# A spectral convolution stage: the next unit's column transforms spread one to a convolution group, with a third PSUM bank, reordered stores and an earlier start

## The chip, the cores and the metric

The kernel runs on one core of one Trainium2 chip. The metric is the device time of one execution in microseconds (us). The median of three executions of the kernel before is 3194.32 us (3190.97 to 3194.67). TensorE is called PE here, VectorE DVE, ScalarE ACT, GpSimd POOL and SyncE SP, as in the profile.

## The reference

Four residual layers act one after the other on x, of shape 8 x 32 x 256 x 256 (batch, channel, height, width), in fp32:

```
x = x + conv0(gn(x))   # spectral: rfft2, mix 32 low and 32 high modes, irfft2, + bias
x = x + conv1(gn(x))   # one 5x5 kernel, each channel on its own, padding 2
x = x + conv2(gn(x))   # a gated recurrence over the 256 columns
x = x + conv3(gn(x))   # running maxima in four directions, then a 1x1 convolution
```

`gn` normalises pairs of channels over the whole image, so a pair's mean and variance must be known before the next layer can use it. The change lies in one function, `inverse_and_conv`, which does the inverse transform of layer 0, adds it to x, takes the statistics of the sum, does layer 1 (the 5x5 convolution) and takes the statistics for layer 2.

## The kernel before, in words

`inverse_and_conv` works through 16 **units** `u`: one image and 16 of its 32 channels each, split in two halves `ch` of 8 channels. A half lives in one of five SBUF buffers `x1_0` to `x1_4`, taken in rotation by `(2u + ch) % 5` (line 340). A buffer has nine column blocks `p` of 32 columns (28 new ones and a rim), and the width is on partitions in four quarters `a` of the image's height.

What a unit needs, step by step:

- `load(u, i)` (381): POOL issues DMAs that fetch x in three pieces of three blocks, two DMAs (one a half) of 768 KB each.
- `load_spectrum(b)` (352): SP issues four DMAs that fetch an image's mixed modes. `spectrum(b)` (362) adds the mean's terms to them on DVE, with one small matmul into the PSUM tag `st`.
- `over_rows` (400): the inverse transform over rows, four calls a unit of 8 PE records in the trace each, PSUM tag `s`; ACT copies the result to `tt`.
- `transform(u, p)` (582) calls `over_columns` (416): the inverse transform over columns for block p, 16 PE records (L424) into two tiles of PSUM tag `up` (two banks), which DVE adds to x (L433) into the x1 buffers. After blocks 2, 5 and 8 it issues the next piece of x for a later unit.
- `squares` (441) and `scale` (452): sums of squares (mostly on ACT), a matmul over them, and on POOL the power that gives the factor `r` of layer 1's normalisation.
- `conv(u, ch, g)` (475): the 5x5 convolution of one channel pair, 36 PE records (L490) into three of four PSUM banks of tag `vp`; five DVE operations (L527) multiply by `r`, add x and sum. A unit has eight such **groups** `g`, four to a half.
- `squares2` (532), `statistics` (552), `keep` (575): layer 2's statistics.
- `store(u, ch)` (541): SP writes a finished half to `x2d` in DRAM in 36 DMAs, four quarters `a` (outer loop) by nine blocks `p` (inner), rows of 256 bytes. Of the very last half, POOL issues 16.

The order of the work is written out by hand (`manual_schedule`, 596): every engine runs its instructions in the order of the program text. Between the groups of unit u stand the column transforms of unit u+1, placed by the tuple

```
PLACES = ((0,), (1, 2), (3, 4), (5, 6), (7,), (8,), (), ())
```

so two transforms follow each other after groups 1, 2 and 3, with a little other PE work between them, and none follows groups 6 and 7. The row transforms of unit u+2 follow groups 3 to 6. `scale(u+1, 0)` comes at the end of unit u. The spectrum of a later image is fetched after group 7 of odd units and prepared after group 2 of the next unit. SP has one queue: stores and spectrum fetches start in program order. A buffer may be overwritten by a later unit's L433 only when the store of its earlier contents has landed: unit u+1's second half takes over the buffer of unit u-1's first half.

After the stage, `recurrence` (672) starts with the transpose of the statistics (L695) and reads `x2d`.

Of the kernel before, what the change touches and what calls it, by code (L numbers as in the profile page):

```python
# [23 lines left out]
A = 4  # L24
# [3 lines left out]
NT = 9  # L28
# [272 lines left out]
def inverse_and_conv(tc, k, d, smd, xmean, x2d, stb, first):  # L301
# [12 lines left out]
    BANKS = ((0, 2), (2, 6), (6, 9))  # L314
    PIECES = ((0, 3), (3, 6), (6, 9))

    PLACES = ((0,), (1, 2), (3, 4), (5, 6), (7,), (8,), (), ())
    with ExitStack() as ctx:
        one = ctx.enter_context(tc.tile_pool(name="a2c", bufs=1))
        xp = ctx.enter_context(tc.tile_pool(name="a2x", bufs=1))  # L320
# [76 lines left out]
                r=[None, None],  # L397
            )

        def over_rows(u, c, tag="s", bufs=1):  # L400


            b, h = units[u]
            tp = ps.tile([P, 2, H], F32, name=f"tp_{u}_{c}", tag=tag, bufs=bufs)
            for j in range(2):
                for ch in range(2):
                    nc.tensor.matmul(
                        tp[64 * ch : 64 * ch + 64, j],
                        lhsT=specs[b][:, 2 * CH * h + CH * ch + c + j].rearrange("p r y -> p (r y)"),
                        rhs=k.eh,  # L410
                        start=True,
                        stop=True,
                    )
            nc.scalar.copy(state[u]["tt"][:, :, c : c + 2, :], tp.rearrange("p c (a q) -> p a c q", a=A))

        def over_columns(u, p, tag="up", bufs=2):


            tt = state[u]["tt"]
            ups = [ps.tile([P, CH * Q], F32, name=f"up_{u}_{p}_{ch}", tag=tag, bufs=bufs) for ch in range(2)]  # L420
            for a in range(A):
                for ch in range(2):
                    r = slice(64 * ch, 64 * ch + 64)
                    nc.tensor.matmul(  # L424
                        ups[ch][32 * a : 32 * a + 32],
                        lhsT=k.gw[r, p, :],
                        rhs=tt[r, a].rearrange("p c q -> p (c q)"),
                        start=True,
                        stop=True,
                    )  # L430
            for ch in range(2):
                free(
                    nc.vector.tensor_tensor(  # L433
                        x1_of(u, ch)[:, p, :, 1 : 1 + Q],
                        ups[ch].rearrange("p (c q) -> p c q", q=Q),
                        xs.pop((u, ch, p)),
                        ALU.add,
                    )
                )
# [32 lines left out]
            if some[0]:  # L472
                tc.declare_no_dep(ins.ins, group="conv", reason="later matmuls of the same bank end last")

        def conv(u, ch, g):

            vps = [
                ps.tile([P, 2 * (hi - lo), Q], F32, name=f"vp_{u}_{ch}_{g}_{lo}", tag="vp", bufs=4) for lo, hi in BANKS
            ]

            def tiles(bank, kind, start=False, stop=False, signal=False, wait=None):
                lo, hi = BANKS[bank]
                for i, r in enumerate(pairs):
                    o = pairs[i if kind == 0 else 1 - i]
                    to = pairs[i if (kind == 0) != (bank == 1) else 1 - i]
                    ins = nc.tensor.matmul(  # L490
                        vps[bank][to],
                        lhsT=k.conv[r, P : P + 64] if kind == 2 else k.conv[r, o],
                        rhs=pair_of(u, ch, g, lo, hi, (2, 0)[i] if kind == 2 else 1, r),
                        start=start,
                        stop=stop,
                    )
                    if wait is not None and i == 0:
                        ins._wait_ge(sem, wait)
                if signal:
                    ins.then_inc(sem, 1)  # L500
                    count[0] += 1
                    tc.add_to_no_dep_group("conv", ins.ins)
                    tc.no_tile_sem_insts.add(ins.ins.name)
                    some[0] = True
                return count[0]

            tiles(1, 1, start=True)
            tiles(2, 1, start=True)
            second = tiles(2, 2, signal=True)
            first = tiles(1, 2, signal=True)  # L510
            tiles(0, 1, start=True)
            tiles(2, 0, stop=True, wait=second)
            third = tiles(0, 2, signal=True)
            tiles(1, 0, stop=True, wait=first)
            tiles(0, 0, stop=True, wait=third)
            s1 = state[u]["s1"]
            everywhere, r1 = slice(0, P), state[u]["r"][ch]
            for n, lo, hi, src, o, rows in (
                (3, 6, 9, vps[2], everywhere, everywhere),
                (2, 2, 6, vps[1], pairs[1], pairs[0]),  # L520
                (2, 2, 6, vps[1], pairs[0], pairs[1]),
                (0, 0, 1, vps[0][:, 0:2], everywhere, everywhere),
                (1, 1, 2, vps[0][:, 2:4], everywhere, everywhere),
            ):
                x = pair_of(u, ch, g, lo, hi, rows=rows)
                free(
                    nc.vector.scalar_tensor_tensor(  # L527
                        x, src[o], r1[rows, g : g + 1], x, ALU.mult, ALU.add, accum_out=s1[rows, 0, n, ch, g : g + 1]
                    )
                )  # L530
# [10 lines left out]
        def store(u, ch):  # L541
            b, h = units[u]
            c0 = 2 * CH * h + CH * ch
            for a in range(A):
                for p, t in enumerate(BLOCKS):
                    lo, hi = 0 if t == 0 else 2, 32 if t == NT - 1 else 30
                    (nc.gpsimd if 2 * u + ch == 2 * n - 1 and p % 2 else nc.sync).dma_start(  # L547
                        out=x2d[b, a, c0 : c0 + CH, TS * t + lo : TS * t + hi].rearrange("c w q -> w c q"),
                        in_=x1_of(u, ch)[32 * a + lo : 32 * a + hi, p, :, 1 : 1 + Q],
                    )  # L550
# [28 lines left out]
                    by_pair(stb[:, kind, b, 2 * CH * h : 2 * CH * (h + 1)]), twice(st[:, kind], 2)  # L579
                )  # L580

        def transform(u, p, again):
            if u:
                over_columns(u, p)
            else:
                over_columns(u, p, "vp", 4)
            if p == 0:
                for ch in range(2):
                    squares(u, ch, 0, 0, 1)
            if again < n:  # L590
                for i, (_, hi) in enumerate(PIECES):
                    if p == hi - 1:
                        load(again, i)

        n = len(units)
        with tc.manual_schedule(engines=None):
# [5 lines left out]
            for u in range(2):  # L602
                begin(u)
            for c in range(0, CH, 2):
                over_rows(0, c, *(("s", 1), ("up", 2))[c // 2 % 2])
            for p in range(NT):
                transform(0, p, 1)
                if p % 2:
                    over_rows(1, p - 1)
                if p == 4:  # L610
                    for ch in range(2):
                        squares(0, ch, 1, 1, 5)
            for ch in range(2):
                squares(0, ch, 2, 5, NT, ch == 1)
                scale(0, ch, 3)
            for u in range(n):
                for g in range(2 * G):
                    conv(u, g // G, g % G)
                    places = PLACES[g] if u + 1 < n else ()
                    for p in places[:1]:  # L620
                        transform(u + 1, p, u + 2)

                    if g == 1 and u > 0:
                        scale(u, 1)
                    if g == 2 and u > 0:
                        st = statistics(u - 1)
                    if g == G - 1 and u + 2 < n:
                        begin(u + 2)
                    if G - 1 <= g < 2 * G - 1 and u + 2 < n:
                        over_rows(u + 2, 2 * (g - G + 1))  # L630
                    for p in places[1:]:
                        transform(u + 1, p, u + 2)
                    squares2(u, g // G, g % G)
                    if g == 2:
                        if u > 0:
                            keep(u - 1, st)
                        if u % 2 == 0 and u + 2 < n:
                            spectrum(units[u + 2][0])
                    if g == 5 and u + 1 < n:
                        squares(u + 1, 0, 1, 1, NT)  # L640
                    if g == 7 and u % 2 and u + 3 < n:
                        load_spectrum(units[u + 3][0])
                    if g % G == G - 1 and (u, g) != (n - 1, 2 * G - 1):
                        store(u, g // G)
                    if u == n - 1 and g == G:
                        nc.gpsimd.dma_start(out=flat(first[:, 0 : B - 1]), in_=first_columns(x2d, 0, B - 1))
                if u + 1 < n:
                    scale(u + 1, 0)
                    squares(u + 1, 1, 1, 1, NT)
            keep(n - 1, statistics(n - 1))  # L650
            store(n - 1, 1)
# [537 lines left out]
```

## Time and profile before

| what | value |
|---|---|
| median of three executions | 3194.32 us |
| the profiled execution | 3195.71 us |
| its span, first to last instruction | 3193.9 us |
| around the span | 1.8 us |
| convolution stage, first column transform to last store issue | 333.6 to 1160.0 us |
| PE busy in 440 to 940 us | 469.57 of 500 us |
| DVE busy in 440 to 940 us | 351.39 of 500 us |
| ACT busy in 440 to 940 us | 293.77 of 500 us |
| mean busy share of the 16 DMA engines in 440 to 940 us | 0.78 |
| DMA share in 1085 to 1125 us, after the last load of x | 0.51 |

How to read it: the profile is of one execution, so sums are made against 3195.71 us. A busy share tells how much of a stretch an engine worked, not whether it set the pace. Time in which SP only waits is not in these rows, so SP has to be read from the order and spacing of its DMA issues.

### The profile page before, as it was taken

How to read it: one execution, taken by the hardware profiler on the slowest of the kernel's cores; microseconds unless marked ns; L12 is line 12 of the kernel's file. 1: busy time of each engine (PE TensorE's matmuls, PEld its weight loads, DVE VectorE, ACT ScalarE, POOL GpSimd, SP SyncE). 2: the span in 40 equal slices, each digit the busy share in tenths (PEclk: the TensorE clock that was granted, in tenths of full speed). 3: DMA queues.
4: the chain of work that ended last, by engine and by line, in shares of the span. 5: the costliest groups of instructions: out<-in, count | busy, mean ns of one | idle time of the engine just before them, and what ended most of it. 6: DMA issues, size and time to landing. Idle time of an engine off the chain costs nothing.

```text
span 3193.9 us, 112013 instructions
## 1 busy us (share of the span) xinstructions
PE 2870.8 (90%) x47802; PEld 1672.7 (52%) x47802; DVE 2589.1 (81%) x5188; ACT 1856.4 (58%) x4362; POOL 862.3 (27%) x1241
## 2 busy tenths in 40 slices
PE   7985799999989969999999999999999678888887
PEld 4655344444434436666666666666666423333333
DVE  5752577777767748999999999999999799999997
ACT  3432365665646657888888888888888412222222
POOL 0110011111111035555555555555555400000000
PEclk9985899999999989999999999999999889999998
DMA  9977577788777655555566655555565588888885
GB/s 384 388 284 200 131 180 202 183 195 196 189 183 184 143 144 142 145 144 145 150 157 160 160 146 146 147 146 146 154 160 134 128 323 321 328 329 329 327 327 233
DMA packets 527057, 655.75 MB, mean 205 GB/s; under 512 B 388824, under 2 KB 389736, under 8 KB 500828
## 3 DMA queue, kind: packets, MB, share of 16 engines
q1 hardware_dynamic: 483628, 494.33, 54.4%
q0 software_dynamic: 17200, 85.05, 8.3%
q10 hardware_dynamic: 25728, 69.21, 5.5%
q8 instruction: 374, 6.13, 0.8%
q14 instruction: 127, 1.04, 0.1%
HBM read 371.63 MB, written 272.63 MB: 202 GB/s over the span
## 4 chain that ended last, share of the span: by engine, by line
PE 60%; DVE 24%; DMA 5%; issue 4%; SPq 4%; ACT 2%; POOL 0%; DVEq 0%; ACTq 0%; POOLq 0%
PE r L742 13%; PE z L742 12%; PE vp L490 8%; PE ni L742 6%; PE nh L742 6%; DVE x L527 4%; DVE rv L1001 4%; PE up L424 4%; SPq L547 3%; PE yp L131 2%; DVE dq L1007 2%; DMA x2d<-x 2%; DVE uq L1009 2%; DVE m L1015 2%; DVE m L1013 2%
## 5 line engine op out<-in xcount | busy, mean ns | idle before, releaser
L750 PE MATMUL z<-hs,weights 64*64 64x256 f32 x4080 | 539.4, 382 | 0.0
L750 PE MATMUL r<-hs,weights 64*64 64x256 f32 x4080 | 525.1, 375 | 0.0
L750 PE MATMUL ni<-hs,weights 64*64 64x256 f32 x4080 | 524.9, 375 | 0.0
L832 POOL TENSOR_TENSOR xw<-xw,hs 128x256 f32<-128x256 f32 x496 | 340.6, 687 | 634.0 <-DVE hs L831 634.0
L527 DVE SCALAR_TENSOR_TENSOR x<-vp,r,x 64x512 f32<-64x512 f32 (+2 forms) x640 | 351.1, 564 | 162.9 <-PE vp L490 136.2
L490 PE MATMUL vp<-x,c_conv 64*64 64x384 f32 (+2 forms) x4608 | 455.7, 513 | 0.2
L1047 ACT ACTIVATE ot<-o,bres 128x512 f32<-128x512 f32 x256 | 155.1, 688 | 505.3 <-PE o L1032 490.3
L826 POOL TENSOR_TENSOR a<-zm,xn 128x256 f32<-128x256 f32 x510 | 373.3, 732 | 6.5 <-issue 6.3
L824 ACT ACTIVATE n<-n,bih 128x256 f32<-128x256 f32 x510 | 259.2, 508 | 185.8 <-DVE n L823 185.8
L490 PEld LDWEIGHTS vp<-x,c_conv 64*64 64x64 f32 x4608 | 237.5, 137 | 232.3 <-issue 126.3
L742 PE MATMUL z<-xn,weights 64*64 64x256 f32 x2040 | 305.3, 376 | 24.1 <-ACT xn L722 24.1
L1032 PE MATMUL o<-m,wsc 32*32 32x512 f32 x3072 | 226.0, 716 | 110.8 <-DVE m L1015 104.0
L742 PE MATMUL r<-hs,weights 64*64 64x256 f32 x2040 | 319.1, 389 | 4.4 <-DVE hs L831 3.4
L742 PE MATMUL r<-xn,weights 64*64 64x256 f32 x2040 | 305.5, 376 | 1.3 <-ACT rs L817 1.3
L742 PE MATMUL nh<-xn,weights 64*64 64x256 f32 x2040 | 305.7, 376 | 0.0
L742 PE MATMUL ni<-hs,weights 64*64 64x256 f32 x2040 | 305.2, 375 | 0.0
L742 PE MATMUL z<-hs,weights 64*64 64x256 f32 x2040 | 305.2, 376 | 0.0
L722 ACT ACTIVATE xn<-xw,shift,turned 128x256 f32<-128x256 f32 x496 | 290.5, 586 | 0.1
L750 PEld LDWEIGHTS ni<-hs,weights 64*64 64x64 f32 x4080 | 284.5, 133 | 0.3
L818 DVE SCALAR_TENSOR_TENSOR n<-nh,bhh,rs 128x256 f32<-128x256 f32 x510 | 246.3, 483 | 45.7 <-ACT rs L817 31.2
L750 PEld LDWEIGHTS r<-hs,weights 64*64 64x64 f32 x4080 | 281.0, 131 | 0.2
L817 ACT ACTIVATE rs<-r,brz 128x256 f32<-128x256 f32 x510 | 241.6, 474 | 53.5 <-PE r L750 31.9
(164 smaller groups left out, 6271.1 us busy)
## 6 DMA issues: line engine op xcount, KB each, us to landing
xb<-in_xl_dram POOLq DMA_DIRECT2D x96, 768.0 KB, 6.5
xa<-in_xt_dram SPq DMA_DIRECT2D x64, 1024.0 KB
x<-x3d SPq DMA_DIRECT2D x32, 2048.0 KB
fw<-fwd SPq DMA_DIRECT2D x32, 2048.0 KB
out_dram<-ot ACTq DMA_DIRECT2D x64, 1024.0 KB
xw<-x2d SPq DMA_DIRECT2D x31, 2048.0 KB
fwd<-fm SPq DMA_DIRECT2D x248, 256.0 KB
x3d<-xw SPq DMA_DIRECT2D x248, 256.0 KB
```

What stands on the lines that cost most here:

```text
L490: ins = nc.tensor.matmul(vps[bank][to], lhsT=k.conv[r, P : P + 64] if kind == 2 else k.conv[r, o], rhs=pair_of(u, ch, g, lo, hi, (2, 0)[i] ...
L527: nc.vector.scalar_tensor_tensor(x, src[o], r1[rows, g : g + 1], x, ALU.mult, ALU.add, accum_out=s1[rows, 0, n, ch, g : g + 1])
L722: nc.scalar.activation(norms[bi][:, b, w], raws[bi][:, b, w], AF.Identity, bias=shift[:, b : b + 1], scale=sc[:, 1, b : b + 1])
L742: ins = nc.tensor.matmul(out[r], lhsT=weights[r, kind, gate, :], rhs=src[r], start=start, stop=stop)
L750: ins = nc.tensor.matmul(out[pairs[1 - i]], lhsT=weights[r, kind, gate, :], rhs=prev[r, :, q0 : q0 + Q], start=False, stop=stop,)
L817: rs = nc.scalar.activation(r, p["r"], AF.Sigmoid, bias=brz[:, 0:1])
L818: nc.vector.scalar_tensor_tensor(m, p["nh"], bhh[:, 2:3], r, ALU.add, ALU.mult)
L824: nc.scalar.activation(m, m, AF.Tanh, bias=bih[:, 2:3])
L826: product = nc.gpsimd.tensor_tensor(a, zm, cur, ALU.mult)
L832: nc.gpsimd.tensor_tensor(raw, raw, new, ALU.add)
L1032: nc.tensor.matmul(pts[b2][i][32 * j : 32 * j + 32].rearrange("p (w q) -> p w q", q=Q), lhsT=wsc[q, b2, t, :], rhs=src[j][q, b2], start=first,
L1047: nc.scalar.activation(ot[:, i], pts[b2][i], AF.Identity, bias=bres[:, b2, i : i + 1])
```

## The change

1. The `up` tag gets three banks in place of two; the tag `s` goes away, and `over_rows` shares the one bank of `st` with the small statistics matmuls.
2. Of unit u+1, transform 0 is issued at the end of group 7 of unit u-1; transforms 1, 2, 3, 5, 6, 7, 8 follow groups 0 to 6 of unit u, and transform 4 stands inside group 3, before the last quarter or so of its matmuls (`between`).
3. `scale(u, 0)` moves from the end of unit u-1 into group 0 of unit u, at the same place inside the group.
4. The squares of unit u+1's first half come in three parts (block 0 after group 1, blocks 1 to 5 after group 4, blocks 6 to 8 before group 7) instead of two; the second half keeps two.
5. `store` loops over blocks outside and quarters inside. Number, size and engine of its DMAs stay as they were.
6. `load_spectrum` moves from after group 7 of odd units to after group 2, and `spectrum` from after group 2 of even units to after group 7 of the odd unit before. `keep` moves from group 2 to group 3.
7. The first `scale`s and transform 0 of unit 1 are put in the same order ahead of unit 0.

```diff
-    PLACES = ((0,), (1, 2), (3, 4), (5, 6), (7,), (8,), (), ())
+    PLACES = (1, 2, 3, 5, 6, 7, 8)
...
-        def over_rows(u, c, tag="s", bufs=1):
+        def over_rows(u, c, tag="st", bufs=1):
...
-        def over_columns(u, p, tag="up", bufs=2):
+        def over_columns(u, p, tag="up", bufs=3):
...
-        def conv(u, ch, g):
+        def conv(u, ch, g, between=()):
...
             third = tiles(0, 2, signal=True)
+            for work in between:
+                work()
             tiles(1, 0, stop=True, wait=first)
...
-            for a in range(A):
-                for p, t in enumerate(BLOCKS):
-                    lo, hi = 0 if t == 0 else 2, 32 if t == NT - 1 else 30
+            for p, t in enumerate(BLOCKS):
+                lo, hi = 0 if t == 0 else 2, 32 if t == NT - 1 else 30
+                for a in range(A):
...
-            for ch in range(2):
-                squares(0, ch, 2, 5, NT, ch == 1)
-                scale(0, ch, 3)
+            for ch in range(2):
+                squares(0, ch, 2, 5, NT, ch == 1)
+            scale(0, 1, 3)
+            transform(1, 0)
             for u in range(n):
+                more, beyond = u + 1 < n, u + 2 < n
                 for g in range(2 * G):
-                    conv(u, g // G, g % G)
-                    places = PLACES[g] if u + 1 < n else ()
-                    for p in places[:1]:
-                        transform(u + 1, p, u + 2)
+                    between = []
+                    if g == 0:
+                        between.append(lambda: scale(u, 0, 3))
+                    if g == 3 and more:
+                        between.append(lambda: transform(u + 1, 4))
+                    if g == 7 and more:
+                        squares(u + 1, 0, 2, 6, NT)
+                    conv(u, g // G, g % G, between)
+                    if g < len(PLACES) and more:
+                        transform(u + 1, PLACES[g])
+                    if g == 2 * G - 1 and beyond:
+                        transform(u + 2, 0)
                     if g == 1 and u > 0:
                         scale(u, 1)
...
-                    for p in places[1:]:
-                        transform(u + 1, p, u + 2)
                     squares2(u, g // G, g % G)
...
+                    if g == 1 and more:
+                        for ch in range(2):
+                            squares(u + 1, ch, 0, 0, 1)
+                    if g == 3 and u > 0:
+                        keep(u - 1, st)
+                    if g == 4 and more:
+                        squares(u + 1, 0, 1, 1, 6)
+                    if u % 2 and u + 3 < n:
+                        if g == 2:
+                            load_spectrum(units[u + 3][0])
+                        elif g == 7:
+                            spectrum(units[u + 3][0])
...
-                if u + 1 < n:
-                    scale(u + 1, 0)
+                if more:
                     squares(u + 1, 1, 1, 1, NT)
```

More of the change, by code (lines that the diff above doesn't have):

```diff
@@ L580, in keep, with transform @@
                 )
-        def transform(u, p, again):
+        def transform(u, p):
             if u:
@@ L586, in transform @@
                 over_columns(u, p, "vp", 4)
-            if p == 0:
+            if u == p == 0:
                 for ch in range(2):
                     squares(u, ch, 0, 0, 1)
-            if again < n:
+            if u + 1 < n:
                 for i, (_, hi) in enumerate(PIECES):
                     if p == hi - 1:
-                        load(again, i)
+                        load(u + 1, i)
         n = len(units)
@@ L604, in inverse_and_conv @@
             for c in range(0, CH, 2):
-                over_rows(0, c, *(("s", 1), ("up", 2))[c // 2 % 2])
+                over_rows(0, c, *(("st", 1), ("up", 3))[c // 2 % 2])
             for p in range(NT):
-                transform(0, p, 1)
+                transform(0, p)
                 if p % 2:
@@ L623, in inverse_and_conv @@
                     if g == 1 and u > 0:
                         scale(u, 1)
[L625 to L630, printed above, removed]
-                    for p in places[1:]:
-                        transform(u + 1, p, u + 2)
-                    squares2(u, g // G, g % G)
@@ L634, in inverse_and_conv @@
                     if g == 2:
                         if u > 0:
-                            keep(u - 1, st)
-                        if u % 2 == 0 and u + 2 < n:
+                            st = statistics(u - 1)
+                        elif beyond:
                             spectrum(units[u + 2][0])
[L639 to L642, printed above, removed]
+                    if g == G - 1 and beyond:
+                        begin(u + 2)
@@ new lines, in inverse_and_conv @@
+                    if G - 1 <= g < 2 * G - 1 and beyond:
+                        over_rows(u + 2, 2 * (g - G + 1))
+                    squares2(u, g // G, g % G)
+                    if g == 1 and more:
[10 more added lines that the diff above has]
+                            spectrum(units[u + 3][0])
```

## The prediction

> **What bounds the kernel now.** I read the busy slices first, then the chain of waits, then PE's timeline through one unit of the convolution stage, and last SP's queue.
>
> ```profile
> PE   7985799999989969999999999999999678888887
> DVE  5752577777767748999999999999999799999997
> DMA  9977577788777655555566655555565588888885
> ...
> PE r L742 13%; PE z L742 12%; PE vp L490 8%; PE ni L742 6%; PE nh L742 6%; DVE x L527 4%; DVE rv L1001 4%; PE up L424 4%; SPq L547 3%; PE yp L131 2%; DVE dq L1007 2%; DMA x2d<-x 2%; DVE uq L1009 2%; DVE m L1015 2%; DVE m L1013 2%
> ```
>
> The stage is slices 5 to 14 of 40. PE is at 9 there and the chain names L490 first, so PE looks like the bound; but SPq L547 and DMA x2d<-x, the stores, are on the chain too. PE through unit 5 (columns: start, length, engine, line, operation, and in brackets the idle time before it with its cause):
>
> ```profile
> 608.34 0.61 PE L457 MATMUL v<-sq,c_valid 128*128 128x4 f32 x4
> 608.88 3.39 PE L490 MATMUL vp<-x,c_conv 64*64 64x512 f32 x36
> 612.20 1.09 PE L424 MATMUL up<-tt,c_gw 64*32 64x512 f32 x16
> ...
> 617.69 0.61 PE L457 MATMUL v<-sq,c_valid 128*128 128x4 f32 x4
> 620.02 2.35 PE L424 MATMUL up<-tt,c_gw 64*32 64x512 f32 x16 [1.72 <-DVE x L433]
> 622.30 4.35 PE L490 MATMUL vp<-x,c_conv 64*64 64x512 f32 x36
> ...
> 637.31 1.68 PE L424 MATMUL up<-tt,c_gw 64*32 64x512 f32 x16 [0.80 <-DVE x L433]
> ```
>
> The second transform of a pair waits for DVE to empty the two `up` banks. Start to next start, the unit's undisturbed pieces are 8 groups x 3.31, 9 transforms x 1.02, 4 row transforms x 1.01, 2 small sums x 0.54 and 1.73 of statistics: 42.6 us. The unit took 48.9 (608.34 to 657.27). The 6.3 missing sit at the pairs: the waits above, transforms stretched to 2.35 and 1.68, and the group after them at 4.35. Were PE all, I would take this off. So SP has to be read:
>
> ```profile
> 390.45 74.11 SPq L547 DMA_DIRECT2D x2d<-x  x108
> 464.66 5.15 SPq L357 DMA_DIRECT2D spec<-smd  x4
> 469.90 94.92 SPq L547 DMA_DIRECT2D x2d<-x  x144
> ...
> 662.34 6.28 SPq L357 DMA_DIRECT2D spec<-smd  x4
> 668.72 91.18 SPq L547 DMA_DIRECT2D x2d<-x  x144
> ...
> 972.86 187.18 SPq L547 DMA_DIRECT2D x2d<-x  x308
> ```
> ```profile
> SPq L547 <- DMA x2d<-x: 65.2, 57, 3.6
> ```
> ```profile
> L547 SPq EVENT_SEMAPHORE  x63: 17/17/17, 328.9 to 1147.7; - x63
> ```
>
> SP's runs of issues touch each other from 390 to 1160 us. What it waits for (second view, 440 to 1083 us) is almost only its own earlier stores. And it is late: unit 2's first half was ready (last L527 of group 3) at 489.2 and its store began at 496.0; unit 6: 686.8 and 691.2; unit 10: 881.9 and 896.0. From unit 1's first store (440.35) to unit 11's (940.08) SP took 499.7 us for ten units, 50.0 each, and never waited for data. PE and DVE took 49.7 a unit (unit 2's group 3 ended at 489.2, unit 13's at 1036.0). The two are level, and **SP's queue is as much the bound as PE**. The next stage needs SP's end, too:
>
> ```profile
>   DMA x2d<-x: 17.6, 1
> ```
>
> That is what DVE waited for ahead of L695, the first step of the recurrence.
>
> **What the Trainium skill says.** "DMA: Bandwidth & Descriptors", section "Queues, rings and completion order": each DMA engine goes round robin between the queues with work, a packet at a time. The trace agrees: POOL's loads went out at 637.6 and had landed at 645.9; of the stores issued from 638.4 none landed before 646.2, after which they landed 0.2 us apart. Outside such bursts a store is issued every 0.46 us and lands in 1.4. The same page, "Latency and other measured facts", gives lower rates for HBM rows a large power of two apart (164 GB/s at 2 MiB and 103 at 4 MiB, against 207 at 512 KiB); no run here shows that yet, and I use it in a rival. "TensorE: Matmul & The Clock Gate", Part 1, has PE's clock halved until it has been busy for about 3.4 us; the trace shows the 4.35 us group after the idle gaps, and a granted clock of 0.83 in 620 to 630 us.
>
> **The change, part by part.**
>
> *Transforms one to a group, third bank (1, 2).* All 9 x 16 transform records of a unit stay. In the order of the built program a transform's first tile takes the free bank, and its second waits for the first L433 of the transform a whole group before. DVE needs 2.86 us for a group's L527 and 1.28 for the adds, 4.1, inside 4.33 (3.31 + 1.02) of PE. So PE's 6.3 us go. If that cover failed, the old 0.6 to 1.7 us a transform would return.
>
> *Scale inside group 0 (3).* The sum's result comes 2.58 + 0.54 us into the group; then DVE 0.15 and POOL 1.0, so the first L527 starts 4.6 us in, not 2.7. DVE falls 1.9 behind; group 1 then waits some 0.2 to 0.4 for a `vp` bank, and DVE catches up in group 2, beside PE's 1.73 of statistics. Cost on PE: 0.4.
>
> *Transform 4 inside group 3* puts its adds (1.3) ahead of that group's L527: DVE 2.2 late, absorbed by the 1.01 of row transforms in each of the next groups: 0. *Squares in three parts (4)*: four more ACT instructions, 4 x (0.31 + 0.19) at most, on an engine busy 294 of 500 us: 0. *Shared `st` bank (1), keep*: users lie in different groups: 0 to 1 us in even units.
>
> So compute asks 42.6 + 0.3 (half a spectrum matmul) + 0.4 = 43.3 us a unit, 6.4 less than now.
>
> *Stores (5) and spectrum (6), SP's queue.* SP still issues 72 stores a unit and 4 fetches every second unit. Its unit: 72 x 0.46 = 33.1; three bursts of loads, which cost 4.1 (638.44 to 646.22 for eight issues instead of 3.7) and 3.8, about 12; a spectrum fetch 5 to 6 us of issue and some 3.5 in the store behind it (25.5 against 22.0), half of that a unit, 4.6. Sum 49.7, against 50.0 measured. Nothing in the change removes an issue or a burst. What the reordering does is to let the next unit start on block p when 4(p+1) stores have landed, not on the 28th. I take SP's work as unchanged; bounds: 0.01 us on or off each of 1152 stores is 11.5 us either way, and a fetch that now falls into a load burst (block 8's load goes out around group 7) may cost or save 2 us, 7 x 2 = 14.
>
> *What is late next:* SP. It falls 6 us a unit further behind, until L433 of block 0 at the end of group 7 waits for the first half's store. That leaves four groups, 22 us, minus four issues and a landing, 3.4: SP may be about 18 us late; the spectrum, due after group 7, allows about 10. From unit 3 or 4 compute is tied to SP, and DVE and PE wait there what they no longer wait at the pairs.
>
> *The sum.* SP is busy from its first store to its last, except for 3.65 us before 440.35 and 2.2 and 2.1 around units 14 and 15: 769.6 - 7.9 = 761.7. These gaps close. The first store starts earlier: unit 0 loses the two pairs in groups 1 and 2 (2.48 each) and a slow group (1.7), 6.7, less 2.2 for transform 4 ahead of L527: 4.5, so at 386 us. End of SP: 386 + 762 = 1148 for 1160, 12 us. The later stages don't change: 3195.7 - 12 = 3183.5 against the profiled execution, which stood 1.4 above the median: about **3182 us**.
>
> **The rivals.**
> 1. *SP's time stretches only because compute is slow; compute sets the pace.* Then 6.4 us x 14 units = 90 us go: 3105; if only the bursts get cheaper by half, 3150. Against it: SP never waits for data and still takes 50.0. For it: the stores' order changes, and after the last load a half takes SP 18 us, not 25.
> 2. *SP's work grows by what it gains*, by fetches caught in bursts (7 x 2 us): 3194, no change.
> 3. *Slower: the order of the stores.* Consecutive stores now go to quarters of x2d 2 MiB apart instead of to neighbouring columns. If that slows the landings after a burst as the skill's page has it, 0.2 us becomes 0.25 (207/164, rows 2 MiB apart) to 0.4 (207/103, 4 MiB apart, as every other quarter is). With 41 pairs of loads after 390 us and 8 stores held by each, 328 landings, that is 16 to 66 us; at 0.3, which I take, 33: 3182 + 33 = 3215. It eats the gain from 12/328 = 0.04 us a landing on, and shows as slower from 0.06. Against it: landings (0.2) are faster than issues (0.46), so some of it hides.
> 4. *The change doesn't do what it says*, that is, pairs keep waiting: excluded by the built order, where no transform waits on one in its own group but transform 5 on 4.
>
> **How the numbers follow.** About 0.2% (6.4 us) is what a measurement of this kernel can tell from no change. SP's work conserved, 3176 to 3188: 0.48, all faster. Rival 1, 3105 to 3170: 0.15, faster. Rival 2, 3188 to 3200: 0.21, same. Rival 3 and its like, above 3200: 0.16. Faster 0.63, same 0.21, slower 0.16. The range leaves out the far half of rival 1 (0.08) and of rival 3 (0.08): 3145 to 3208.
>
> **What would show it.** Right: SP's runs still touch from about 386 us to about 1148; units 1 to 3 take 43 to 45 us on PE, later ones about 50; waits of L433 on DMA x2d or of the spectrum's steps on DMA spec appear, tens of us in sum; L695 comes 12 us earlier. Wrong: units of 43 us to the end with SP waiting for data (rival 1), or stores whose landings are more than 0.2 us apart after a burst (rival 3).

## The result: 0.1% less time, not clear of no change, where 0.4% was forecast

| kernel | median, us | runs | lowest to highest |
|---|---|---|---|
| before | 3193.22 | 12 | 3186.41 to 3206.98 |
| changed | 3189.61 | 12 | 3184.57 to 3194.65 |

The ratio is 0.9989, with a 95% interval of 0.9977 to 1.0002. A second series, told below, gave 0.9990 (0.9979 to 1.0002). The forecast of 3182 lies 7.6 us under the median; the wide range of 3145 to 3208 held it. By the prediction's own bound of 0.2% the outcome is "same", to which it gave 0.21, and not "faster", to which it gave 0.63: 3189.6 lies 1.6 us outside its 3176 to 3188 for SP's work conserved, in the stretch of rival 2.

The changed kernel's profiled execution took 3185.27 us with a span of 3183.4. The busy slices and the chain of waits, from its page:

```profile
PE   7975798988889949999999999999999678888887
DVE  5742576766667738999999899999989799999997
DMA  9977578777787646555556665555565588888885
...
PE r L756 13%; PE z L756 12%; PE vp L490 9%; PE ni L756 6%; PE nh L756 6%; SPq L549 5%; DVE rv L1015 4%; DMA x2d<-x 3%; PE up L424 3%; PE yp L131 3%; DVE dq L1021 2%; DVE uq L1023 2%; DVE m L1029 2%; DVE m L1027 2%; DVE m L1025 2%
```

PE's digits in the stage are no higher than before, some are lower, and the hole in the slice at its end is deeper (4 in place of 6). `SPq L549`, the stores (L547 before), went from 3% of the chain to 5%, and `DMA x2d<-x` from 2% to 3%. SP's timeline (start, length, engine, line, operation):

```profile
382.69 46.19 SPq L549 DMA_DIRECT2D x2d<-x  x72
428.97 10.38 SPq L357 DMA_DIRECT2D spec<-smd  x4
439.45 95.97 SPq L549 DMA_DIRECT2D x2d<-x  x144
535.52 9.67 SPq L357 DMA_DIRECT2D spec<-smd  x4
...
944.89 203.85 SPq L549 DMA_DIRECT2D x2d<-x  x344
```

The runs touch from 382.7 to 1148.7 us, and only the first half's store began as soon as the half was ready: all later ones were late. What DVE and PE wait for in 400 to 1050 us (total, times, longest):

```profile
DVE x L433 <- DMA x2d<-x: 62.0, 9, 12.9
PE y L367 <- DMA spec<-smd: 49.4, 5, 10.5
DVE x L433 <- PE up L424: 29.3, 13, 2.3
```

The same window in the kernel before:

```profile
DVE x L433 <- PE up L424: 44.9, 39, 2.0
PE up L424 <- DVE x L433: 36.1, 39, 4.4
DVE x L433 <- DMA x2d<-x: 5.9, 1, 5.9
```

PE's waits for DVE at the pairs are gone. DVE's 29.3 us for `up` are now 13 waits of 2.3 us, all for transform 4, which stands inside group 3 ahead of that group's L529. Waits for SP's transfers stand in place of the rest. Where they are is seen in PE's timeline from the end of unit 5 into unit 6:

```profile
634.10 3.38 PE L490 MATMUL vp<-x,c_conv 64*64 64x512 f32 x36
637.41 1.09 PE L424 MATMUL up<-tt,c_gw 64*32 64x512 f32 x16
646.47 0.61 PE L367 MATMUL y<-spec,c_dc 128*128 128x32 f32 x2 [7.98 <-DMA spec<-smd]
647.01 4.80 PE L490 MATMUL vp<-x,c_conv 64*64 64x512 f32 x28
```

After the last group PE is at the spectrum's small matmul, but SP, which still had older stores to issue, began to fetch it only at 634.37. On DVE, in the same place, block 0's add waits for a store:

```profile
648.61 0.69 DVE L433 TENSOR_TENSOR x<-up,xb 128x512 f32<-128x512 f32 x1 [8.34 <-DMA x2d<-x]
```

The next stage shows it once more. In 1050 to 1165 us DVE waits for the last stores ahead of the recurrence's first step (L709, L695 before):

```profile
DVE turned L709 <- DMA x2d<-x: 32.3, 1, 32.3
```

It waited 17.6 us there before. Compute finished its last unit some 26 us earlier and waited 15 of them out: L709 starts at 1150.5, where L695 started at 1161.8.

### The profile page after: what moved, and what is told of

Read it like the earlier page. It is cut to its first block, busy times and chain, and to the rows that moved or that the text cites. A ratio compares the mean times of both kernels' runs of the same rounds, so it can differ in the third digit from the quotient of the medians.

```text
span 3183.4 us, 112304 instructions
## 1 busy us (share of the span) xinstructions
PE 2839.0 (89%) x47832; PEld 1663.1 (52%) x47832; DVE 2586.2 (81%) x5188; ACT 1874.2 (59%) x4482; POOL 860.1 (27%) x1241
## 4 chain that ended last, share of the span: by engine, by line
PE 63%; DVE 19%; SPq 7%; DMA 6%; issue 4%; ACT 1%; POOL 0%; DVEq 0%; ACTq 0%; POOLq 0%
PE r L756 13%; PE z L756 12%; PE vp L490 9%; PE ni L756 6%; PE nh L756 6%; SPq L549 5%; DVE rv L1015 4%; DMA x2d<-x 3%; PE up L424 3%; PE yp L131 3%; DVE dq L1021 2%; DVE uq L1023 2%; DVE m L1029 2%; DVE m L1027 2%; DVE m L1025 2%
## 5 line engine op out<-in xcount | busy, mean ns | idle before, releaser
L490 PE MATMUL vp<-x,c_conv 64*64 64x256 f32 (+2 forms) x4608 | 459.8, 504 | 2.4 <-DVE x L529 2.3
L529 DVE SCALAR_TENSOR_TENSOR x<-vp,r,x 64x512 f32<-64x512 f32 (+2 forms) x640 | 350.8, 563 | 98.9 <-PE vp L490 68.2
L490 PEld LDWEIGHTS vp<-x,c_conv 64*64 64x64 f32 x4608 | 224.1, 134 | 207.8 <-issue 114.5
L536 ACT ACTIVATE junk<-x 128x128 f32<-128x128 f32 (+1 forms) x384 | 202.9, 528 | 145.0 <-DVE x L529 136.1
```

Source lines behind the costliest of these rows:

```text
L490: ins = nc.tensor.matmul(vps[bank][to], lhsT=k.conv[r, P : P + 64] if kind == 2 else k.conv[r, o], rhs=pair_of(u, ch, g, lo, hi, (2, 0)[i] ...
L529: nc.vector.scalar_tensor_tensor(x, src[o], r1[rows, g : g + 1], x, ALU.mult, ALU.add, accum_out=s1[rows, 0, n, ch, g : g + 1])
L536: nc.scalar.activation(junk[:, : 2 * (hi - lo)], pair_of(u, ch, g, lo, hi), AF.Square, accum_out=state[u]["s1"][:, 1, n, ch, g : g + 1],)
```

## The experiments

The theory is that two chains are level, compute (PE with DVE) and SP's stores, and that the change shortens the first alone. The main rivals are that compute sets the pace, or that the order of the stores or the new place of the spectrum's fetch gives back what the transforms gain.

### A third of the stores issued by POOL, before and after

```diff
-                    (nc.gpsimd if 2 * u + ch == 2 * n - 1 and p % 2 else nc.sync).dma_start(
+                    (nc.gpsimd if (p % 2 if 2 * u + ch == 2 * n - 1 else p % 3 == 2) else nc.sync).dma_start(
```

The changed kernel with this edit:

> The changed kernel, with a third of the stores (blocks with p % 3 == 2) issued by POOL in place of SP. Theory (SP's queue of stores, held up by the bursts of loads, sets the pace of the convolution stage): SP keeps 48 stores a unit, 48 x 0.46 + 12 for bursts + 4.6 for the spectrum = 38.7 us, less than the 43.3 that compute asks, so the waits on x2d and on the spectrum go, units take 43 to 45 us to the end, and the stage ends some 60 to 80 us earlier: about 3190 - 70 = 3120 us. Rival (compute, PE and DVE together, can't go faster than about 49 us a unit for long): no gain, 3185 to 3195. Rival (the DMA engines themselves are full, no matter who issues): little gain, 3175 to 3190.

The kernel before with it:

> The kernel before, with the same third of the stores issued by POOL. Theory: SP is no longer late, but the pairs of transforms still cost 6 us a unit, so units stay at 48.3 to 50.1 us and only the stalls behind late stores and SP's tail go: 10 to 25 us faster than before, 3170 to 3183. Rival (compute is not the second bound; stores alone set the pace): as far down as the changed kernel with the same edit, about 3120.

Measured: 3193.7 us, ratio to before 1.0005 (0.9993 to 1.0016), and 3296.3, ratio 1.0325 (1.0302 to 1.0349). The first gained nothing and the second lost 3.2%. What SP, DVE and POOL wait for in the changed kernel with a third on POOL (SP in 440 to 1050 us, the others in 400 to 1050):

```profile
SPq L549 <- DVE x L529: 192.4, 27, 17.2
SPq L549 <- DMA x2d<-x: 8.0, 13, 1.2
```
```profile
DVE x L529 <- POOL r L463: 72.4, 13, 6.4
POOL x2d L549 <- DMA xb<-in_xl_dram: 40.1, 29, 3.2
```

SP was relieved: it waited 192 us for data. But POOL also computes `r` (L463), and POOL's timeline shows it behind a whole batch of stores:

```profile
602.37 7.47 POOL L549 DMA_DIRECT2D x2d<-x  x12 [2.14 <-DVE x L529]
609.86 1.03 POOL L463 TENSOR_TENSOR r<-ve,c_mhalf 128x4 f32<-128x4 f32 x1
```

Twelve issues of 0.62 us each (SP's median was 0.42) stand ahead of a scale that DVE needs. In the kernel before with this edit the same wait is longer still:

```profile
DVE x L527 <- POOL r L463: 93.9, 12, 9.2
```

A new wait took the old one's place, so this pair doesn't decide on the theory.

### Part 5 undone: quarters outside again

```diff
-            for p, t in enumerate(BLOCKS):
-                lo, hi = 0 if t == 0 else 2, 32 if t == NT - 1 else 30
-                for a in range(A):
+            for a in range(A):
+                for p, t in enumerate(BLOCKS):
+                    lo, hi = 0 if t == 0 else 2, 32 if t == NT - 1 else 30
```

> The changed kernel with the old loop order of the stores (quarters outside, blocks inside), part 5 undone. Theory: SP's work is the same, the next unit's block 0 now waits for the 28th store and not for the 4th, so compute is tied to SP with less room but SP still never runs dry: within 6 us of the changed kernel, rather slower, 3186 to 3196. Rival (stores that go to quarters 2 MiB apart land more slowly, and that ate the gain): faster than the changed kernel by 8 us or more, 3175 to 3182.

Measured: 3196.2 us, ratio 1.0018 (1.0011 to 1.0026). DVE's wait for stores at block 0, in 400 to 1050 us, is longer than the changed kernel's 62.0:

```profile
DVE x L433 <- DMA x2d<-x: 72.0, 9, 13.4
```

The new order of the stores is a gain of about 0.3%, so rival 3 falls. Nor did the landings move apart: where no store had landed for over 2.5 us, the next ones landed 0.21 us apart in the changed kernel and 0.23 in the kernel before (medians, from the completion signals in 440 to 940 us). The Trainium skill ("DMA: Bandwidth & Descriptors", "Latency and other measured facts") has lower rates where the rows of one copy, of 16 KiB each, lie 2 MiB apart. Here it is consecutive stores that do, with rows of 256 bytes, and no loss is seen.

### Part 6 undone: the spectrum at its old place

```diff
-                        elif beyond:
+                        if u % 2 == 0 and beyond:
                             spectrum(units[u + 2][0])
...
-                        if g == 2:
+                        if g == 7:
                             load_spectrum(units[u + 3][0])
-                        elif g == 7:
-                            spectrum(units[u + 3][0])
```

> The changed kernel with the spectrum fetched after group 7 and prepared after group 2 of the next unit as before, part 6 undone. In the changed kernel's profile PE waits 49 us for the fetch ahead of L367. Theory: those waits are only the place where compute is held by SP; they move to L433 on x2d and the time stays within 6 us of the changed kernel, 3184 to 3196. Rival (the fetch, now due earlier, is itself what ate the gain): 20 to 50 us faster, 3140 to 3170.

Measured: 3182.1 us, ratio 0.9972 (0.9962 to 0.9983), against 0.9989 for the whole change. This is below the 3184 to 3196 that I expected, and far from the rival's 3140 to 3170. The intervals overlap; the ratios put part 6 at a loss of some 0.17%, 5 us. The profiled execution was the slowest of the eleven (3188.2), so its trace can't show where they would come from. A fetch still took SP 10.9 us there with the store behind it (8.9 in the kernel before, 12.0 in the changed one), so its place is not the main thing that made it longer.

### Loads by block: SP's stalls taken away

The stores stall behind POOL's loads, so the loads were cut. x is fetched in nine pieces of one block, two DMAs of 256 KB each, in place of three pieces with two of 768 KB. So the loads are smaller, and they also go out at nine points of a unit in place of three. Bytes, stores and compute stay.

```diff
-    PIECES = ((0, 3), (3, 6), (6, 9))
+    PIECES = tuple((p, p + 1) for p in range(NT))
...
-            for i in range(3):
+            for i in range(len(PIECES)):
                 load(0, i)
```

The changed kernel with it:

> The changed kernel with x loaded block by block: nine pairs of 256 KB loads a unit in place of three pairs of 768 KB, so PIECES has nine pieces of one block. Bytes, buffers and stores stay. Theory (SP's eight stores in flight stand still while a pair of large loads drains, 8 us each time, of which only 8 x 0.46 = 3.7 us are covered): a pair a third as long, some 2.7 us, is covered by the eight in flight, SP's unit falls from 50 to about 40 us, and compute at 43 to 45 us a unit sets the pace: 50 to 75 us faster, 3115 to 3140. Rival (the DMA engines' total work, bytes and packets, sets the pace): no change, 3183 to 3195; more packets, rather slower. Rival (compute can't go faster for other reasons): no change, and SP waits for data.

The kernel before with it:

> The kernel before with the same edit of PIECES. Theory: SP is relieved as well, but the pairs of transforms keep compute at 48.3 to 50.1 us a unit, so 5 to 20 us faster than before: 3172 to 3187. What the changed kernel gains beyond that is what the spread transforms are worth once SP is out of the way. Rival (stores alone set the pace in both): as fast as the changed kernel with this edit.

Measured, as ratios to the kernel before:

| | loads of three blocks | loads by block |
|---|---|---|
| pairs of transforms (before) | 1 | 0.9988 (0.9979 to 0.9996), 3183.5 us |
| one transform to a group (changed) | 0.9989 (0.9977 to 1.0002), 3189.6 us | 0.9820 (0.9803 to 0.9837), 3126.9 us |

Each edit alone brings some 0.1% at most; together they bring 1.8%. SP's waits in 440 to 1050 us, first the changed kernel, then the changed kernel with loads by block, then the kernel before with loads by block:

```profile
SPq L549 <- DMA x2d<-x: 63.3, 50, 3.3
```
```profile
SPq L549 <- DVE x L529: 16.3, 17, 4.7
SPq L549 <- DMA x2d<-x: 10.7, 26, 1.2
```
```profile
SPq L547 <- DVE x L527: 53.6, 15, 7.1
SPq L547 <- DMA x2d<-x: 18.0, 32, 1.1
```

SP's wait for its own earlier stores falls from 63.3 to 10.7 us. In the kernel before it then waits 53.6 us for data, so compute is the bound, and the pairs' waits are still there in 400 to 1050 us:

```profile
DVE x L433 <- PE up L424: 43.7, 39, 2.0
PE up L424 <- DVE x L433: 29.1, 32, 1.5
```

In the changed kernel with loads by block SP's ten units from 437.67 take 46.0 us each (50.5 without):

```profile
437.67 83.90 SPq L549 DMA_DIRECT2D x2d<-x  x144
521.67 8.20 SPq L357 DMA_DIRECT2D spec<-smd  x4
...
897.77 192.49 SPq L549 DMA_DIRECT2D x2d<-x  x344
```

This decides between the theory and rival 1. The work of the DMA engines as a whole isn't the bound either: the bytes are the same, and the engines' busy share in 440 to 940 us rises from 0.77 to 0.90. Nor did compute wait for x: in 400 to 1050 us of the changed kernel no L433 waited for a load. The change is worth 56.6 us here (3183.5 to 3126.9) and a few behind the stalled SP. Whether the size of the loads or their spacing relieves SP isn't told apart.

### Loads by block and the old place of the spectrum

The edits of the last two sections together.

> The changed kernel with both edits: loads by block, and the spectrum fetched after group 7 and prepared after group 2 as in the kernel before (part 6 undone), which alone was 0.28% faster than before. Theory: SP no longer lags, so the place of the fetch matters little: within 8 us of the run with loads by block alone. Rival (the late fetch holds compute whatever SP does): 10 us or more slower than that run, since spectrum is then due only three groups after its fetch is issued.

Measured: 3122.3 us, ratio 0.9802 (0.9785 to 0.9819). It was 0.9820 without the second edit: a gain of the same sign as above, but the intervals overlap. SP's unit is 45.3 us.

### The changed kernel again

No edit; a second series against the kernel before.

> The changed kernel unchanged, for a second profile and a tighter interval. Theory: 0.1 to 0.3% faster than before, 3181 to 3188, with SP's runs of issues touching from about 383 to 1150 us and the spectrum fetches taking 9 to 10 us each where the kernel before took 5 to 6. Rival (the first profile was a lucky one and the change gives nothing): ratio 0.999 to 1.001, stage end at 1155 to 1160.

Measured: 3185.6 us in 13 runs against 3188.0 in 25, ratio 0.9990 (0.9979 to 1.0002). Stores went out from 384.3 to 1152.5 us, 768.1 us, and again the runs of issues touch.

### Loads by block, two banks

Part 1 undone in the kernel of 3126.9 us; the transforms stay one to a group.

```diff
-        def over_rows(u, c, tag="st", bufs=1):
+        def over_rows(u, c, tag="s", bufs=1):
...
-        def over_columns(u, p, tag="up", bufs=3):
+        def over_columns(u, p, tag="up", bufs=2):
...
-                over_rows(0, c, *(("st", 1), ("up", 3))[c // 2 % 2])
+                over_rows(0, c, *(("s", 1), ("up", 2))[c // 2 % 2])
```

> The kernel with loads by block (3126.9 us), with two `up` banks in place of three, and the row transforms back in a bank of their own; one transform to a group stays. My theory (third bank needed): a transform's tiles then take both banks in turn, and each may start only when DVE has added the tile of the transform before; since that was a whole group earlier, the wait is mostly covered, but DVE runs its adds behind the group's five operations, so I expect 0.3 to 0.6 us of wait at most transforms, nine a unit, 14 units: 30 to 60 us over 3126.9, that is 3157 to 3187. Rival: it is the single placement alone that removes the waits, and the third bank adds nothing: within 8 us of 3126.9.

Measured: 3124.9 us, ratio 0.9783 (0.9769 to 0.9798). My theory fell: no gain from the third bank shows. (The median is 2 us below that with three banks and the ratio 0.4% lower; the two come from different series, in which the kernel before stood at 3192.9 and 3188.0, so I don't read a loss from it.) In 440 to 1050 us two banks show on PE's weight loads:

```profile
PEld up L424 <- DVE x L433: 21.1, 37, 0.8
```

With three banks it is 10.5 us in 13 waits, so two more transforms a unit wait, at most 0.8 us each. From the first L529 of one group to that of the next, the step over group 3, with transform 4 inside, grew from 4.41 to 4.90 us, and no other by more than 0.3. The placement alone removes the pairs' waits.

### Loads by block, quarters outside

Part 5 undone in the kernel of 3126.9 us, by the edit shown above.

> The kernel with loads by block, with the old order of the stores (quarters outside, blocks inside). Behind a late SP queue the old order cost 6.5 us (3196.2 against 3189.6). My theory: with loads by block SP still runs 6 to 10 us late, so the wait of block 0 for the 28th store in place of the 4th (24 issues of 0.46 us, 11 us later) shows in most units, some us each: 3130 to 3150. Rival: SP is early enough in this kernel for the order not to matter: within 4 us of 3126.9.

Measured: 3168.8 us, ratio 0.9926 (0.9903 to 0.9949), 1.1% above loads by block alone (1.3% by the medians). I had expected 0.1 to 0.7%. DVE's and SP's waits in 440 to 1050 us show a ring:

```profile
DVE x L433 <- DMA x2d<-x: 42.8, 6, 8.4
```
```profile
SPq L549 <- DVE x L529: 43.9, 17, 5.0
```

DVE waits for stores and SP, with no stall left, waits for DVE. Quarters outside hold a block until the 28th store of the half; odd units, where a fetch stands ahead of that half, took 15.0 us over their last group, where loads by block with the new order took 9.05. The order of the stores matters to the spread transforms: block 0 of the next unit is now wanted a group earlier. So over half of the 56.6 us that the change is worth with small loads (34 by the ratios, 42 by the medians) needs part 5 as well: the placement removes the pairs' waits, and the new order keeps them from coming back as waits for stores.

### Loads by block, the old spectrum, a few stores on POOL

In the kernel of 3122.3 us POOL issues the last two blocks of each first half, 8 of the 72 stores of a unit, when it has no scale to compute.

```diff
-                    (nc.gpsimd if 2 * u + ch == 2 * n - 1 and p % 2 else nc.sync).dma_start(
+                    (nc.gpsimd if (p % 2 if 2 * u + ch == 2 * n - 1 else ch == 0 and p >= 7) else nc.sync).dma_start(
```

> Loads by block and the old place of the spectrum (3122.3 us), and 8 of the 72 stores of a unit, the last two blocks of its first half, issued by POOL instead of SP. My theory: SP's unit falls from 45.3 us by 8 x 0.46 = 3.7 to 41.6 us, below the 43.3 that compute asks, so compute sets the pace: 14 units x 2.0 = 28 us less, about 3095, and up to 3115 where POOL's own turn is late. Rival: compute, not SP, already sets the pace of 45.3 (short waits that add up), or POOL's stores delay what stands behind them: 3118 to 3130, no gain.

Measured: 3115.0 us, ratio 0.9755 (0.9739 to 0.9771), the fastest of all and at the upper end of what I expected. SP now waits for data, 49.9 us in 440 to 1050:

```profile
SPq L549 <- DVE x L529: 49.9, 24, 5.2
SPq L549 <- DMA x2d<-x: 14.9, 32, 1.3
```

Units (first L529 to first L529) take 43.5 us without a spectrum and 44.7 to 47.8 with one, 45.1 in the mean of units 2 to 12: compute sets the pace.

### The spectrum fetched by ACT

This was to relieve SP in the changed kernel with the loads as they are.

```diff
-                    nc.sync.dma_start(
+                    (nc.sync if b < 2 else nc.scalar).dma_start(
                         out=t[64 * ri : 64 * ri + 64, :, ro], in_=smd[b, ri ^ ro].rearrange("s x o y -> (s x) o y")
```

> The changed kernel with its six later spectrum fetches (24 DMAs) issued by ACT instead of SP, at the same place in the order; loads, stores and everything else stay as they are, and the same bytes move. My theory (SP's queue of issues is the bound): SP loses six fetches of 9.7 us, 58 us of its 766, and the stage ends some 50 to 58 us earlier, 3131 to 3140. Rival (the 16 DMA engines or the loads themselves are the bound, and SP's queue only shows it): the fetches take their share of the DMA engines all the same, and the time stays within 10 us of 3189. A third case: ACT stands in the fetch for up to 10 us, and the sums of squares or the row transforms behind it come late: some 10 to 20 us of the gain are lost again, 3140 to 3160.

Measured: 3194.0 us, ratio 1.0023 (1.0009 to 1.0036): the rival's number, but not for the rival's reason. What SP waits for in 440 to 1050 us:

```profile
SPq L549 <- DMA spec<-smd: 82.2, 16, 17.2
SPq L549 <- DMA x2d<-x: 63.0, 47, 3.0
```

SP waits 82 us for fetches that it no longer issues. In the trace the store that goes out at 621.74, after a pause from 606.82, has the completion signal (a semaphore that tells of the landing) that the first of ACT's fetch DMAs took at 617.03. SP's stores and ACT's fetches share eight such signals in turn in this build, and the store that was next on this one went out only when ACT's fetch had. 58 us of issues were taken from SP and a longer wait was put in. What SP's queue without the fetches would bring under the large loads stays open; a run with signals kept apart wasn't tried.

## Why the prediction was right, and where it was off

*SP's queue is as much the bound as PE*: right. The table of four kernels shows it: either chain alone freed brings 0.1% at most, both 1.8%.

*The pairs' 6.3 us go, and compute asks 43.3 us*: right for the placement. The first two units took 42.6 and 43.8 us on PE (from one unit's first convolution matmul to the next's) before SP caught them. The "free bank" of the argument, the third one, was not needed. One term was mis-sized: the spectrum was put at 0.3 us a unit, its matmul; all its steps lengthen every second unit by 3.0 us (46.5 in the mean against 43.5, in the fastest kernel, where no wait for a fetch is left), 1.5 a unit.

*SP falls behind until compute is tied to it*: right. The lag from the last L529 of a half to its first store rose to 13 to 27 us (18 was estimated), and units from the fourth to the fourteenth took 45 to 55 us, 49.8 in the mean of units 2 to 12. Nearly all of the wait sits at the end of odd units, behind a fetch.

*The sum.* The mechanism held; the size of the gain did not, 3.6 us between the medians for the 12 of the forecast. The terms against the two profiled executions of the changed kernel:

| term | predicted, us | first | second |
|---|---|---|---|
| first store | 386 | 382.7 | 384.3 |
| SP's work to the last store | 761.7 | 766.0 | 768.1 |
| last store | 1148 | 1148.7 | 1152.5 |
| profiled execution | 3183.5 | 3185.27 | 3189.53 |

The step that was off is "I take SP's work as unchanged": it grew by 4.3 to 6.4 us, inside the 11.5 that the prediction left open. Within it two terms moved in opposite directions. A fetch with the store behind it took 12.0 us of SP in place of 8.9, over six fetches (not the seven I counted) 19 us; the other issues gave most of it back, and a store's issue was 0.515 us in the mean of 440 to 940 us, 0.538 before. The first is rival 2's mechanism, but what makes the fetch longer isn't settled, since with the fetch at its old place it is 10.9 us. With part 6 undone the kernel was 0.28% faster than before, nearer to the forecast; that part 6 took the difference is not shown, as the intervals overlap.

The second error is the yardstick. The profile of before (3195.71 us) stood 1.4 above the median of three runs, but 2.5, 5.0 and 7.7 above the medians of 12, 38 and 25 later runs. Of the 12 us, 10.4 and 6.2 appeared between profiled executions, and 3.6 and 2.4 between medians. The first profile of the changed kernel stood 4.3 below its median and the second 3.9 above, so it is partly luck that the first comes within 2 us of 3183.5. The kernel before spreads over some 20 us from run to run, and a sum made on one execution inherits that.

Rival 1 was refuted for this kernel, and its 3105 nearly appeared once SP was out of the way (3115). Rival 2 was right in part: SP's work grew, by a third to a half of what was to be gained, and not by all. Rival 3 was refuted in sign. Rival 4 was refuted by the first units.

## What to carry to other kernels

When two chains are level, removing either one's waits shows almost nothing, and the edit looks worthless; free both, one at a time and together, before judging it. A queue that never waits for data but waits for its own earlier transfers can be a bound even where an engine is over 90% busy, as PE was here. Ask what holds those transfers: here large loads on another queue, and cutting them in three cost nothing.

## What the runs showed of the hardware

- A load of 768 KB landed 6.4 us (median) after its issue and one of 256 KB after 3.8, both in 440 to 940 us. The small ones took most of the stores' stalls away (63.3 to 10.7 us), at three times the number of loads and the same bytes.
- A store's issue took 0.62 us on POOL and 0.42 (median) on SP.
- A DMA moved from SP's queue to ACT's still held SP up, through completion signals that the two share: 82 us in 16 waits.
